# A two-layer graph attention kernel: the last head's aggregation in seven products, and layer 2's logits and softmax in another order

## The chip, the cores and the metric

The kernel runs on one core of a Trainium2 chip. The metric is the device time in microseconds. The engines that matter are TensorE (PE, matrix products; PEld is its weight load), VectorE (DVE), ScalarE (ACT), GpSimd (POOL, used here to issue accumulating DMAs) and SyncE (SP, which issues the plain DMAs). Each engine works through its own list of instructions in order.

## The reference

Everything is fp32. There are 512 nodes with 768 features, and 16,896 edges with self loops. `x` goes through two graph attention layers, and the result is the layer norm of `x` plus the second layer's output:

```python
def gat_layer(x, W, a_s, a_d, b, edge_index, concat):
    h = (x @ W).reshape(n, H, C)
    alpha_s = einsum('nhc,hc->nh', h, a_s)
    alpha_d = einsum('nhc,hc->nh', h, a_d)
    e = leaky_relu(alpha_s[src] + alpha_d[dst], 0.2)
    e = exp(e - segment_max(e, dst)[dst])
    alpha = e / (segment_sum(e, dst)[dst] + EPS)
    out = segment_sum(h[src] * alpha[:, :, None], dst)
    return out + b

h = elu(gat_layer(x, W1, ...))        # 8 heads of 768
out = gat_layer(h, W2, ...)           # 1 head of 768, from 8 x 768
x = layernorm(x + out)
```

The kernel turns the edge list into a 512 x 512 matrix of counts once, and then every attention is a dense softmax over 512 sources, with the counts folded in, followed by a dense product.

## The kernel before

**Stages.** A head of layer 1 has four: its projection (`x` times a 768 x 768 block of W1), its logits and softmax (which give `PT`, the transposed attention), its aggregation (the projected features times `PT`, then bias and ELU, which gives `gT`: 6 chunks of 128 features by 512 nodes), and its product with a 768 x 768 block of W2, which is added to `h2`, the features of layer 2. Heads overlap: while TensorE multiplies for one, VectorE and ScalarE do another's softmax. The loop over `h` ends with head 6, whose second product covers head 7's softmax. What stands behind the loop is head 7's aggregation and second product, then layer 2's logits, softmax, aggregation and layer norm, in one list.

**Products with fewer multiplications.** Most products are cut in two or three in each dimension and done in Strassen's manner, with sums of blocks ahead and sums of results behind. In halves there are seven products, P1 to P7, and four sums of blocks on each side. `mixed` does so for the aggregation of heads 0 to 6. It takes a pair of feature chunks (c and c+3) at a time: seven products of two matmuls of 128x128 by 128x256, in the order P1, P6, P7, P2, P5, P4, P3. P2 is added over P1's bank, P4 over P7's, P3 over P5's. ScalarE copies P1 into `u`; VectorE adds P6 to give the next `u`, P7 to give `w`, and makes both halves of `zr` and the last `u` from P5, P4 and P3. `elu` is three ScalarE instructions (Relu, Relu, Exp) and one on VectorE that writes `gT`. `left_sums` and `right_sums` make the sums for it. `second` does the last head's product with W2 in fourteen steps (seven products, two row tiles each), every step three matmuls of 384 columns, each with an emptying step: P1 goes to `u2` and P6 is added to it; P2, P7, P4, P5 and P3 go to `h2`; `fold` adds `u2` to the quarters of `h2` that want it.

**The last head** is aggregated plainly by `aggregate`: for each of six feature chunks, four matmuls of 128x128 by 128x512, and an ELU over all 512 nodes.

**Banks.** The pool `mm` has five banks of PSUM in rotation. A product that starts a bank waits until the engine that read the last one there is done.

**The order is written out by hand.** The program is scheduled manually: each engine runs its instructions in the order in which the Python issues them. In the loop, `plan` says what is issued behind the n-th of the fifteen products of `second_by_thirds` and ahead of its emptying: `score(t)` (lift: ScalarE spreads a tile's logits), `scored(t)` (`leak` and `rank` on VectorE, the exponential on ScalarE), `out_by_dma(t)` (scale, and a DMA transposition on SP's queue), `turn_in(t)` (ScalarE puts the transposed tile into `PT`). Tiles 2 and 3 of head 7 are transposed on TensorE by `turn`. Outputs in `by_dma` are emptied by ScalarE into a buffer of `pass_` or `absent` and added to `h2` by an accumulating DMA of POOL.

**Behind the loop, before.** `last_sum` (a POOL DMA) completes one weight sum of W2's last block. `right` gives two further sums, `t2` and `t4`, on VectorE. Eight logit rows of `h2` (`logits`, VectorE) lie between the aggregation's chunks. Layer 2's logits are linear in `h2`, so the last head's share comes from `V` times `gT` instead of from `h2`: `add_rows` multiplies two columns of weights by `gT`, in column tiles of TensorE 32 wide, up to four at a time, and adds `al2`, the logits of `h2` so far, in tile 2. `picks` spreads the resulting rows (`BC[H]`, `own`), and the softmax of layer 2 goes on beside the remaining ten products, one tile per two products. The last stage multiplies `PT` by `h2` for four node tiles, in two or three column pieces each, and VectorE adds the residual, takes the statistics and normalises.

Of the kernel before, what the change touches and what calls it, by code (L numbers as in the profile page):

```python
# [8 lines left out]
F32 = mybir.dt.float32  # L9
# [28 lines left out]
def gat_pass(  # L38
# [421 lines left out]
    def by_thirds(dest, A_, B_, order, fresh, by_dma=()):  # L460

        bank, begun, free = {}, set(), list(passed)

        def out(o):
            return dest[:, 2 * o[0]:2 * o[0] + 2, o[1] * TH:(o[1] + 1) * TH]

        def step(p):
            chain, o, sign = STEPS[p]
            copied = fresh and o not in begun
            begun.add(o)  # L470

            def multiply(between=None):
                first = chain not in bank
                if first:
                    bank[chain] = mm.tile([P, 512], F32, name="mm")
                for i in range(2):
                    for k in range(2):
                        if between and i == k == 1:
                            between()
                        nc.tensor.matmul(bank[chain][:, i * TH:(i + 1) * TH], A_[p][:, k, i * P:(i + 1) * P], B_[p][:, k, :],  # L480
                                         start=first and i == k == 0, stop=k == 1, skip_group_check=True)

            def empty():
                ps = bank[chain].rearrange("p (i n) -> p i n", i=2)
                if copied:
                    nc.scalar.activation(out(o), ps, AF.Copy, scale=sign)  # L486
                elif o in by_dma:
                    free.append(free.pop(0))
                    part = free[-1].rearrange("p (i n) -> p i n", i=2)
                    nc.scalar.activation(part, ps, AF.Copy, scale=sign)  # L490
                    nc.gpsimd.dma_start(out(o), part, accum_op=ALU.add)  # L491
                else:
                    nc.vector.tensor_tensor(out(o), out(o), ps, op=ALU.add if sign > 0 else ALU.subtract)  # L493
            return multiply, empty

        return [step(p) for p in order]
# [6 lines left out]

    def second_by_thirds(h, A_, B_):
        return by_thirds(h2, A_, B_, ("P13", "P2", "P8", "P4", "P12", "P9", "P6", "P0", "P1", "P14", "P10", "P5", "P11", "P7", "P3"),
                         False, ((1, 2), (0, 0), (0, 2)) if h + 2 < H else ((1, 2), (0, 0)))

    def second(A_, B_):

        bank = {}  # L510

        def pair(p, i, start, acc, new):
            def multiply(between=None):
                if start:
                    bank[i] = mm.tile([P, 512], F32, name="mm")
                product(bank[i], A_, B_, p, i, start, between)

            def empty():
                a, ps = acc(i), bank[i][:, :HALF]
                if new:  # L520
                    nc.vector.tensor_scalar(a, ps, 1.0, None, op0=ALU.mult)
                else:
                    nc.vector.tensor_tensor(a, a, ps, op=ALU.subtract if p == "P7" else ALU.add)
            return multiply, empty

        steps = [
            ("P1", True, lambda i: u2[:, i, :], True),
            ("P2", False, lambda i: h2[:, i, L], False),
            ("P6", True, lambda i: u2[:, i, :], False),
            ("P7", True, lambda i: h2[:, 2 + i, R], False),  # L530
            ("P4", False, lambda i: h2[:, 2 + i, L], False),
            ("P5", True, lambda i: h2[:, 2 + i, R], False),
            ("P3", False, lambda i: h2[:, i, R], False),
        ]
        return [pair(p, i, *rest) for p, *rest in steps for i in range(2)]
# [378 lines left out]
        nc.scalar.activation(neg, neg, AF.Exp, scale=-1.0)  # L914
        return lambda: nc.vector.scalar_tensor_tensor(gT[:, c, cols], neg, -1.0, pos, op0=ALU.add, op1=ALU.add)

    def aggregate(h, c):

        ps = mm.tile([P, 512], F32, name="mm")
        for s in range(NT):  # L920
            nc.tensor.matmul(ps[:, :N], HS[h][:, s, c * P:(c + 1) * P], PT[:, s, :],  # L921
                             start=(s == 0), stop=(s == NT - 1))
        return elu(h, c, ps[:, :N], slice(0, N), "r")

    near, far_ = slice(0, HN), slice(HN, N)

    def left_sums(h):
        hs = HS[h]  # L930
        a11, a12, a21, a22 = hs[:, :2, L], hs[:, 2:, L], hs[:, :2, R], hs[:, 2:, R]
        s1, s2, s4 = (gS.rearrange("p a k n -> p a (k n)")[:, j, :].rearrange("p (k n) -> p k n", k=2)
                      for j in range(3))
        tt = nc.vector.tensor_tensor
        return dict(P1=a11, P2=a12, P3=s4, P4=a22, P5=s1, P6=s2, P7=a21), [
            lambda: tt(s1, a21, a22, op=ALU.subtract),
            lambda: tt(s2, s1, a11, op=ALU.subtract),
            lambda: tt(a21, a11, a21, op=ALU.subtract),
            lambda: tt(s4, a12, s2, op=ALU.add),
        ]  # L940
# [12 lines left out]
    def mixed(h, A_, B_, fill, ends=()):  # L953
# [4 lines left out]
        def some(c, j):  # L958
            for f in fill[c][j]:
                f()  # L960

        for c in range(HK):
# [32 lines left out]
            for f in list(ends[1:]) * (c == HK - 1):  # L995
                f()
            tt(u, part("P3", over="P5"), u, op=ALU.subtract)
            some(c, 1)

            def others(c=c, u=u, zr=zr):  # L1000
# [116 lines left out]
    for h in range(H - 1):  # L1117
# [63 lines left out]
        else:  # L1181
# [27 lines left out]
            if last:  # L1209
                plan = {0: finish[:1], 1: finish[1:] + sum_up("P12") + at(score, 0), 2: sum_up("P9", "P7"), 3: sum_up("P1"),  # L1210
                        4: sum_up("P6") + at(scored, 0) + at(score, 1), 5: sum_up("P14"), 6: sum_up("P10") + at(scored, 1) + at(score, 2),
                        7: at(out_by_dma, 0) + sum_up("P5"), 8: sum_up("P11") + at(scored, 2) + at(score, 3), 9: at(out_by_dma, 1),
                        10: at(scored, 3), 11: at(scale, 2) + sum_up("P3"), 12: third_sum + at(scale, 3), 13: at(turn_in, 0) + at(turn_in, 1)}
            behind_it = {1: of_b("P7")}

            def also(n, *what):
# [55 lines left out]
        elif not last:  # L1272
            B_, sums = right(W1[h + 2], "w2")
            pairs = projection(h + 2, XA, B_)
            for n in range(14):
# [23 lines left out]
                if n == 13:  # L1299
                    late_["P10"]()  # L1300
                    behind = [late_["P8"]]
                    in_second, in_third = [late_["P13"], late_["P9"]], {2: late_["P12"], 7: late_["P5"]}
        else:
            last_sum()
            B2, sums2 = right(W2[H - 1], "w1")

# [3 lines left out]
    AL[H] = (al2[:, 0, :], al2[:, 1, :])  # L1312
    GA, gsums = left(gT, gS)
    nc.vector.tensor_tensor(V[:, :, 1], V[:, :, 1], V2, op=ALU.add)
    finish = []
    parts = [(h2[:, 2 + i, L], i, ALU.add) for i in range(2)] + [
        (h2[:, j + i, R], i, ALU.subtract) for j in (2, 0) for i in range(2)]

# [1 line left out]
        for part, i, op in parts:  # L1320
            nc.vector.tensor_tensor(part, part, u2[:, i, :], op=op)

    for c in range(DC):
        finish.append(aggregate(H - 1, c))
        if c:
            finish.pop(0)()
        if 0 < c < 5:
            logits(H, h2, c - 1)
        if c in (2, 4):
            sums2.pop(0)()  # L1330

    rows = tr.tile([P, 512], F32, name="tr")
    nc.vector.memset(rows, 0.0)

    def add_rows(lhsT, rhs, j, cols, start, stop):
        nc.tensor.matmul(rows[32 * j:32 * j + 2, cols], lhsT, rhs, start=start, stop=stop,
                         tile_position=(0, 32 * j), skip_group_check=True)

    every = slice(0, N)
    pairs = second(GA, B2)  # L1340
    pairs[0][0]()
    for c in range(4):
        add_rows(V[:, c, :], gT[:, c, :], c, every, True, c == 3)
    pairs[1][0]()
    pairs[0][1]()
    finish.pop(0)()
    for c in (4, 5):
        add_rows(V[:, c, :], gT[:, c, :], c - 4, every, False, True)
    for t in range(NT):
        add_rows(al2[:, :, t], ident, 2, slice(t * P, (t + 1) * P), False, t == NT - 1)  # L1350
    row2 = work.tile([P, N], F32, name="nr")
    nc.scalar.copy(row2, rows[:, :N])
    gsums[0]()
    gsums[1]()
    pairs[1][1]()
    pairs[2][0]()
    BC[H] = bc.tile([P, 512], F32, name="bc")
    nc.tensor.matmul(BC[H][:, :N], picks[:, 0:1].to_broadcast([P, P]), row2, start=True, stop=True)
    own = tr.tile([P, 512], F32, name="tr")
    for t in range(NT):  # L1360
        nc.tensor.matmul(own[:, t:t + 1], row2[:, t * P:(t + 1) * P], picks[:, 1:2], start=True, stop=True)
    gsums[2]()
    pairs[3][0]()
    gsums[3]()
    nc.vector.tensor_copy(own2, own[:, :NT])
    AL[H] = (None, own2)
    pairs[2][1]()
    pairs[3][1]()
    q, rden = [lift(H, 0)], []
    for n in range(2, 7):  # L1370
        (m0, e0), (m1, e1) = pairs[2 * n:2 * n + 2]
        m0()
        m1()
        if n < 6:
            leak(q[n - 2])
            rank(q[n - 2], n - 2)
        if n < 5:
            q.append(lift(H, n - 1))
        if n < 6:
            e0()  # L1380
        if n > 2:
            rden.append(weigh(q[n - 3], n - 3, scale=False))
            if n > 4:
                turn_in(n - 5)
            turn_out(q[n - 3], n - 3)
        if n == 6:
            fold(parts[2:4])
            e0()
        e1()
        if n == 2:  # L1390
            fold(parts[:2])
    fold(parts[4:])


# [71 lines left out]
```

## Time and profile before

| | |
|---|---|
| median of 3 runs | 634.85 us (634.31 to 635.33) |
| the profiled execution, its own time | 634.52 us |
| its span, first to last instruction | 632.7 us |
| TensorE busy | 621.1 us (98%) |
| VectorE busy | 520.1 us (82%) |
| ScalarE busy | 333.1 us (53%) |
| head 6's aggregation, seven products | 507.53 to 525.66 us |
| head 7's aggregation, plain | 552.97 to 573.84 us |
| its second product, with layer 2's softmax | 573.84 to 605.03 us |
| the last aggregation and layer norm | 605.03 to 632.7 us |
| granted TensorE clock, mean | 0.998 |

Times in the trace are microseconds from the start of the span. A row of the timeline has start, length, engine, line of the kernel, operation, output and inputs with their shapes, a count, and in brackets the engine's idle time before the row and what ended it. An fp32 matmul leaves two records, so 24 matmuls show as x48. Lengths of instructions in a queue overlap a little: the next one starts before the end of the last is recorded.

### The profile page before, as it was taken

The page shows a single profiled execution, that of the slowest core. Times are in us where ns is not written, and L with a number is a line of the kernel's source. Part 1 is how long each engine was busy: PE and PEld are TensorE (multiplying, and loading weights), DVE is VectorE, ACT ScalarE, POOL GpSimd, SP SyncE. Part 2 cuts the span into 40 slices and gives each one's busy share as a digit, 9 for nine tenths or more (in the row PEclk, how much of TensorE's full clock was granted, in tenths as well). Part 3 has the DMA queues.
Part 4 walks back from the last instruction along what each step waited for, and adds up shares of the span by engine and source line. Part 5 has one row for each costly group of instructions (what it writes and reads, how often), then busy time and mean ns, then how long its engine had stood idle before and what let it go on. Part 6 is the DMA issues. An engine that isn't in the chain of part 4 may idle for free.

```text
span 632.7 us, 8415 instructions
## 1 busy us (share of the span) xinstructions
PE 621.1 (98%) x2725; PEld 476.6 (75%) x2725; DVE 520.1 (82%) x1106; ACT 333.1 (53%) x585; POOL 148.6 (23%) x176
## 2 busy tenths in 40 slices
PE   8999999999999999999999999999999999999995
PEld 5555586556888888888888888888888888845553
DVE  8979989788898888968897878968896878756775
ACT  5874775640658246751658146751758056743440
POOL 1300011023342323323333432313342303110000
PEclk9999999999999999999999999999999999999999
DMA  8993397789999998999899998999899995270122
GB/s 307 327 235 91 73 256 254 174 240 264 235 209 155 317 256 184 188 275 222 225 225 201 295 249 199 172 286 239 209 219 217 284 283 86 51 179 1 33 59 79
DMA packets 108752, 127.36 MB, mean 201 GB/s; under 512 B 41574, under 2 KB 89886, under 8 KB 107934
## 3 DMA queue, kind: packets, MB, share of 16 engines
q1 hardware_dynamic: 74718, 90.17, 46.5%
q0 software_dynamic: 33552, 35.99, 37.2%
q10 hardware_dynamic: 432, 0.59, 0.3%
q8 instruction: 24, 0.39, 0.2%
q14 instruction: 26, 0.21, 0.1%
HBM read 98.66 MB, written 2.90 MB: 161 GB/s over the span
## 4 chain that ended last, share of the span: by engine, by line
PE 85%; DVE 7%; DMA 4%; ACT 2%; issue 1%; SPq 1%; DVEq 0%; POOLq 0%; ACTq 0%
PE mm L480 39%; PE mm L974 17%; PE mm L409 17%; PE mm L921 3%; PE mm L1412 3%; DMA w2r<-in_L_gnn_W_dram 3%; PE held L409 2%; PE tr L742 1%; DMA w2t<-in_L_gnn_a_dst_dram 1%; DVE h L493 1%; DVE q L640 1%; DVE q L645 1%; DVE hs L1073 1%; PE bc L276 1%; PE held L608 1%
## 5 line engine op out<-in xcount | busy, mean ns | idle before, releaser
L486 ACT ACTIVATE hs<-mm 128x512 f32<-128x512 f32 x30 | 17.9, 596 | 88.6 <-PE mm L480 70.5
L974 PE MATMUL mm<-PT,hs 128*128 128x256 f32 x252 | 61.3, 379 | 0.0
L493 DVE TENSOR_TENSOR hs<-hs,mm 128x512 f32<-128x512 f32 x45 | 30.8, 684 | 27.6 <-PE mm L480 27.6
L649 ACT ACTIVATE q<-q,nmax 128x512 f32<-128x512 f32 x32 | 23.1, 721 | 57.3 <-DVE nmax L645 57.3
L974 PEld LDWEIGHTS mm<-PT,hs 128*128 128x128 f32 x252 | 47.8, 190 | 7.2 <-ACT u L978 0.3
L491 POOL DMA_DIRECT2D h<-pass x23 | 27.7, 1313 | 94.7 <-ACT pass L490 85.8
L493 DVE TENSOR_TENSOR h<-h,mm 128x512 f32<-128x512 f32 x55 | 37.6, 684 | 9.6 <-PE mm L480 9.0
L974 PE MATMUL mm<-pS,gS 128*128 128x256 f32 x168 | 43.1, 379 | 0.0
L903 ACT COPY PT<-zr 128x1024 uint16<-128x1024 uint16 x34 | 39.1, 1155 | 2.4 <-DMA zr<-pS 1.8
L480 PE MATMUL mm<-w2r,gT 128*128 128x256 f32 x160 | 37.9, 385 | 0.0
L480 PE MATMUL mm<-w2r,xT 128*128 128x256 f32 x160 | 37.8, 379 | 0.0
L133 POOL DMA_DIRECT2D w1t<-in_L_gnn_W_dram x18 | 28.9, 1632 | 31.4 <-DMA w1t<-in_L_gnn_W_dram 29.6
L974 PEld LDWEIGHTS mm<-pS,gS 128*128 128x128 f32 x168 | 31.9, 190 | 4.3
L480 PE MATMUL mm<-w1t,hs 128*128 128x256 f32 x144 | 34.2, 380 | 0.5 <-DVE h L493 0.5
L480 PEld LDWEIGHTS mm<-w2r,gT 128*128 128x128 f32 x160 | 29.6, 190 | 6.6 <-DVE hs L493 3.0
L480 PE MATMUL mm<-w1r,hs 128*128 128x256 f32 x144 | 34.0, 379 | 0.0
L480 PE MATMUL mm<-w1r,gS 128*128 128x256 f32 x144 | 34.0, 379 | 0.0
L480 PEld LDWEIGHTS mm<-w2r,xT 128*128 128x128 f32 x160 | 30.4, 190 | 4.1
L978 ACT COPY u<-mm 128x256 f32<-128x256 f32 x21 | 7.8, 371 | 45.7 <-PE mm L974 45.7
L480 PEld LDWEIGHTS mm<-w1t,hs 128*128 128x128 f32 x144 | 27.2, 190 | 4.7 <-DVE h L493 0.9
L716 DVE TENSOR_SCALAR os<-nodes,idx 128x512 bf16<-128x512 f16 x104 | 29.0, 352 | 1.4 <-PE tr L742 1.4
L480 PEld LDWEIGHTS mm<-w1r,gS 128*128 128x128 f32 x144 | 27.3, 190 | 3.7
(282 smaller groups left out, 1544.8 us busy)
## 6 DMA issues: line engine op xcount, KB each, us to landing
w2r<-in_L_gnn_W_dram SPq DMA_DIRECT2D x48, 384.0 KB
w1r<-in_L_gnn_W_dram SPq DMA_DIRECT2D x43, 384.0 KB
gT<-xd SPq DMA_DIRECT2D x5, 1280.0 KB
w1t<-in_L_gnn_W_dram SPq DMA_DIRECT2D x24, 256.0 KB
h<-pass POOLq DMA_DIRECT2D x23, 256.0 KB, 4.7
w1t<-in_L_gnn_W_dram POOLq DMA_DIRECT2D x18, 256.0 KB, 6.1
w2t<-in_L_gnn_W_dram SPq DMA_DIRECT2D x15, 256.0 KB
w2t<-in_L_gnn_W_dram POOLq DMA_DIRECT2D x15, 256.0 KB, 8.9
```

What stands on the lines that cost most here:

```text
L133: nc.gpsimd.dma_start(o, i, accum_op=ALU.add)
L409: nc.tensor.matmul(ps[:, :HALF], A_[p][:, k, i * P:(i + 1) * P], B_[p][:, k, :], start=start and k == 0, stop=k == HK - 1, skip_group_chec ...
L480: nc.tensor.matmul(bank[chain][:, i * TH:(i + 1) * TH], A_[p][:, k, i * P:(i + 1) * P], B_[p][:, k, :], start=first and i == k == 0, stop= ...
L486: nc.scalar.activation(out(o), ps, AF.Copy, scale=sign)
L491: nc.gpsimd.dma_start(out(o), part, accum_op=ALU.add)
L493: nc.vector.tensor_tensor(out(o), out(o), ps, op=ALU.add if sign > 0 else ALU.subtract)
L649: nc.scalar.activation(q, q, AF.Exp, bias=nmax, scale=-1.0, accum_out=dens[t])
L716: nc.vector.tensor_scalar(o, nodes, idx[:, c:c + 1], None, op0=ALU.is_equal)
L903: nc.scalar.copy(PT.rearrange("p s n -> p (s n)").bitcast(U16).rearrange("p (s n h) -> p s n h", s=NT, h=2)[:, :, t * P:(t + 1) * P, :], p ...
L921: nc.tensor.matmul(ps[:, :N], HS[h][:, s, c * P:(c + 1) * P], PT[:, s, :], start=(s == 0), stop=(s == NT - 1))
L974: nc.tensor.matmul(bank[p][:, :HN], A_[p][:, k, c * P:(c + 1) * P], B_[p][:, k, :], start=over is None and k == 0, stop=k == 1, skip_group ...
L1412: nc.tensor.matmul(ps[:, :cols.stop - cols.start], PT[:, s, t * P:(t + 1) * P], h2[:, s, cols], start=(s == 2), stop=(s == 1))
```

## The change

The last head is aggregated by a new function, `last_mixed`, in seven products of halves for three pairs of chunks. It differs from `mixed` in the order. P1 of chunks 0 and 1 and P2 of chunks 0 and 1 come first, since they need no sums. Then P6, P7, P5, P4, P3 of chunk 0, the same five of chunk 1, and all seven of chunk 2 with P2 between P7 and P5. The four right sums and one left sum are issued on VectorE ahead of everything; the three other left sums are issued in the last steps of head 6's second product. One of them lies in `pass_`, and so head 6's output P7 no longer goes through `pass_` and a POOL DMA, but is added by VectorE.

The sums `t2` and `t4` of W2's last block are made by two loads on SP and two accumulating DMAs on POOL, as for the first heads (`sums_by_dma`). `second` empties P1 by a ScalarE copy instead of a VectorE one.

Layer 2's work is issued in another order. One logit row and then two are issued inside chunk 2 of the aggregation, the other five inside the second product. The six `gT` rows are issued together, in three column tiles, behind the third product; the `al2` rows behind the seventh product, alone; `picks` inside the eighth. The softmax starts behind the eighth product instead of the fourth.

```diff
-                elif o in by_dma:
+                elif p in by_dma:
...
-                         False, ((1, 2), (0, 0), (0, 2)) if h + 2 < H else ((1, 2), (0, 0)))
+                         False, ("P13", "P2", "P8", "P0", "P7", "P3") if h + 2 < H else ("P13", "P2", "P8", "P0"))
...
-                    nc.vector.tensor_scalar(a, ps, 1.0, None, op0=ALU.mult)
+                    nc.scalar.copy(a, ps)
...
-    def left_sums(h):
+    def left_sums(h, ends=None):
...
+        if ends is not None:
+            s2 = ends[:, :D].rearrange("p (k n) -> p k n", k=2)
...
+    def last_mixed(A_, B_, sums, fill):
+
+        h, tt = H - 1, nc.vector.tensor_tensor
+        banks, us, nears = {}, {}, {}
...
+        def begin(c):
+            us[c] = work.tile([P, HN], F32, name="u")
+            nc.scalar.copy(us[c], part(c, "P1"))
+
+        def near_half(c):
+            nears[c] = elu(h, c, part(c, "P2", "P1"), near, "l")
...
+        for f in sums:
+            f()
+        for c in range(2):
+            begin(c)
+        for c in range(2):
+            near_half(c)
+        behind = []
+        for c in range(HK):
+            if c == 2:
+                begin(c)
+            u, w, zr = us[c], work.tile([P, HN], F32, name="w"), work.tile([P, N], F32, name="zr", bufs=3)
+            if behind:
+                behind = behind[0]()
+            tt(u, u, part(c, "P6"), op=ALU.add)
+            if c == 0:
+                nears[0]()
+            tt(w, u, part(c, "P7"), op=ALU.add)
+            for f in behind[:1]:
+                f()
+            if c == 2:
+                near_half(c)
+            some(c, 0)
+            tt(zr[:, far_], part(c, "P5"), w, op=ALU.subtract)
+            for f in behind[1:]:
+                f()
+            tt(zr[:, near], u, part(c, "P4", "P7"), op=ALU.add)
+            if c:
+                nears[c]()
+            tt(u, part(c, "P3", "P5"), u, op=ALU.subtract)
+            some(c, 1)
...
-                        10: at(scored, 3), 11: at(scale, 2) + sum_up("P3"), 12: third_sum + at(scale, 3), 13: at(turn_in, 0) + at(turn_in, 1)}
+                        10: at(scored, 3), 11: at(scale, 2) + sum_up("P3"), 12: third_sum + at(turn_in, 0) + at(scale, 3), 13: at(turn_in, 1)}
+                AA, lsums = left_sums(H - 1, pass_.rearrange("p j n -> p (j n)"))
+                plan[13] += lsums[:2]
+                plan[14] = lsums[2:3]
...
+            B2, additions = sums_by_dma(W2[H - 1], w2[(H - 1) * D:, :], "w1")
+            additions[0]()
             last_sum()
-            B2, sums2 = right(W2[H - 1], "w1")
+            additions[1]()
...
-    for c in range(DC):
-        finish.append(aggregate(H - 1, c))
...
+    BB, rsums = right_sums()
+    finish = last_mixed(AA, BB, [*rsums, lsums[3]], {(1, 0): [lambda: nc.vector.memset(rows, 0.0)], (2, 0): second_[:1], (2, 1): first})
...
+    run(pairs[0][0], pairs[0][1], pairs[1][0], pairs[1][1], *finish, gsums[0], gsums[1], pairs[2][0], pairs[2][1])
+    for c in range(DC):
+        add_rows(V[:, c, :], gT[:, c, :], c % 3, every, c < 3, c > 2 and c % 3 != 2)
+    run(second_[1], pairs[3][0], gsums[2], pairs[3][1], *third_, pairs[4][0], *fourth, pairs[5][0], pairs[4][1], pairs[5][1], gsums[3],
+        pairs[6][0])
     for t in range(NT):
         add_rows(al2[:, :, t], ident, 2, slice(t * P, (t + 1) * P), False, t == NT - 1)
     row2 = work.tile([P, N], F32, name="nr")
     nc.scalar.copy(row2, rows[:, :N])
...
+    fold(parts[:2])
...
+    pairs[7][0](pick)
     nc.vector.tensor_copy(own2, own[:, :NT])
...
+    score(0)
+    run(pairs[6][1], pairs[7][1], pairs[8][0], pairs[9][0])
+    scored(0)
+    score(1)
+    pairs[8][1]()
+    weighed(0)
+    run(pairs[9][1], pairs[10][0], pairs[11][0])
+    scored(1)
+    score(2)
+    pairs[10][1]()
+    weighed(1)
+    scored(2)
+    score(3)
+    run(pairs[11][1], pairs[12][0], pairs[13][0])
+    turn_in(0)
+    weighed(2)
+    fold(parts[2:4])
+    scored(3)
+    pairs[12][1]()
+    turn_in(1)
+    weighed(3)
+    pairs[13][1]()
     fold(parts[4:])
```

In this list a step `pairs[n][0]` is a product, `pairs[n][1]` its emptying; `pairs[0]` and `[1]` are P1, `[2]` and `[3]` P2, then P6, P7, P4, P5, P3. `weighed(t)` takes the reciprocal of a tile's sum and sends the tile to its DMA transposition.

More of the change, by code (lines that the diff above doesn't have):

```diff
@@ L915, in elu @@
         return lambda: nc.vector.scalar_tensor_tensor(gT[:, c, cols], neg, -1.0, pos, op0=ALU.add, op1=ALU.add)
[L917 to L923, printed above, removed]
     near, far_ = slice(0, HN), slice(HN, N)
-    def left_sums(h):
+    def left_sums(h, ends=None):
         hs = HS[h]
@@ L997, in mixed, with others, part, some @@
             tt(u, part("P3", over="P5"), u, op=ALU.subtract)
+            some(c, 1)
+            def others(c=c, u=u, zr=zr):
+                return [elu(h, HK + c, zr, slice(0, N), "r", spare=zr), elu(h, c, u, far_, "l", spare=u)]
+            behind = [others]
+        return behind[0]()
+    def last_mixed(A_, B_, sums, fill):
+        h, tt = H - 1, nc.vector.tensor_tensor
+        banks, us, nears = {}, {}, {}
+        def part(c, p, over=None):
+            if over is None:
+                banks[c, p] = mm.tile([P, 512], F32, name="mm")
+            else:
+                banks[c, p] = banks[c, over]
+            for k in range(2):
+                nc.tensor.matmul(banks[c, p][:, :HN], A_[p][:, k, c * P:(c + 1) * P], B_[p][:, k, :],
+                                 start=over is None and k == 0, stop=k == 1, skip_group_check=True)
+            return banks[c, p][:, :HN]
+        def begin(c):
[3 more added lines that the diff above has]
+            nears[c] = elu(h, c, part(c, "P2", "P1"), near, "l")
+        def some(c, j):
+            for f in fill.get((c, j), ()):
+                f()
[23 more added lines that the diff above has]
+            for f in behind[1:]:
+                f()
+            tt(zr[:, near], u, part(c, "P4", "P7"), op=ALU.add)
+            if c:
+                nears[c]()
+            tt(u, part(c, "P3", "P5"), u, op=ALU.subtract)
             some(c, 1)
@@ L1314, in gat_pass @@
     nc.vector.tensor_tensor(V[:, :, 1], V[:, :, 1], V2, op=ALU.add)
-    finish = []
     parts = [(h2[:, 2 + i, L], i, ALU.add) for i in range(2)] + [
@@ L1321, in fold @@
             nc.vector.tensor_tensor(part, part, u2[:, i, :], op=op)
-    for c in range(DC):
-        finish.append(aggregate(H - 1, c))
[L1325 to L1330, printed above, removed]
     rows = tr.tile([P, 512], F32, name="tr")
-    nc.vector.memset(rows, 0.0)
     def add_rows(lhsT, rhs, j, cols, start, stop):
@@ L1337, in add_rows, with given, run @@
                          tile_position=(0, 32 * j), skip_group_check=True)
+    def given(t):
+        return [lambda al=al, a=a, sign=sign: nc.vector.scalar_tensor_tensor(
+            scr, h2[:, t, :], sign, a, op0=ALU.mult, op1=ALU.mult, accum_out=al[:, t:t + 1])
+            for al, a, sign in zip(AL[H], A[H], (1.0, -1.0))]
+    first, second_, third_, fourth = (given(t) for t in range(NT))
+    BB, rsums = right_sums()
+    finish = last_mixed(AA, BB, [*rsums, lsums[3]], {(1, 0): [lambda: nc.vector.memset(rows, 0.0)], (2, 0): second_[:1], (2, 1): first})
     every = slice(0, N)
     pairs = second(GA, B2)
[L1341 to L1348, printed above, removed]
+    def run(*fs):
+        for f in fs:
+            f()
+    run(pairs[0][0], pairs[0][1], pairs[1][0], pairs[1][1], *finish, gsums[0], gsums[1], pairs[2][0], pairs[2][1])
[3 more added lines that the diff above has]
+        pairs[6][0])
     for t in range(NT):
@@ L1352, in gat_pass, with pick, weighed @@
     nc.scalar.copy(row2, rows[:, :N])
[L1353 to L1358, printed above, removed]
-    own = tr.tile([P, 512], F32, name="tr")
[L1360 to L1364, printed above, removed]
+    fold(parts[:2])
+    own = tr.tile([P, 512], F32, name="tr")
+    def pick():
+        BC[H] = bc.tile([P, 512], F32, name="bc")
+        nc.tensor.matmul(BC[H][:, :N], picks[:, 0:1].to_broadcast([P, P]), row2, start=True, stop=True)
+        for t in range(NT):
+            nc.tensor.matmul(own[:, t:t + 1], row2[:, t * P:(t + 1) * P], picks[:, 1:2], start=True, stop=True)
+    pairs[7][0](pick)
     nc.vector.tensor_copy(own2, own[:, :NT])
     AL[H] = (None, own2)
[L1367 to L1391, printed above, removed]
+    q, rden = {}, {}
+    def weighed(t):
+        rden[t] = weigh(q[t], t, scale=False)
+        turn_out(q[t], t)
+    h = H - 1
+    score(0)
[20 more added lines that the diff above has]
+    pairs[13][1]()
     fold(parts[4:])
```

## The prediction

> **What bounds the kernel now.** I read the page first, then the chain of work that ended last, then the timeline around the last two heads.
>
> ```profile
> span 632.7 us, 8415 instructions
> ...
> PE 621.1 (98%) x2725; PEld 476.6 (75%) x2725; DVE 520.1 (82%) x1106; ACT 333.1 (53%) x585; POOL 148.6 (23%) x176
> ```
>
> TensorE is busy nearly all the time, so what counts is its work and the moments when it stands. The chain says where:
>
> ```profile
> 507.53 18.13 PE mm L974 x84
> ...
> 552.97 20.87 PE mm L921 x48
> 573.84 1.94 PE mm L409 x6
> 575.77 0.97 PE tr L1336 x8
> 576.75 2.13 PE mm L409 x6
> 578.88 0.98 PE tr L1336 x8
> 579.86 2.13 PE mm L409 x6
> 581.99 0.86 PE bc L1358 x2
> 582.85 0.79 PE tr L1361 x8
> 583.63 21.39 PE mm L409 x66
> 605.03 19.80 PE mm L1412 x64
> ```
>
> The columns are start, length, and what ran. One earlier head's aggregation, already in seven products (L974), is 18.13 us. The last head's, in plain form (L921), is 20.87. From 552.97 to 605.03, 52.06 us, the chain never leaves TensorE: aggregation, then fourteen products of layer 2 (L409, three matmuls each, 21.39/11 = 1.945 us where eleven follow each other), and the small matmuls of L1336, L1358 and L1361 between them. The last aggregation (L1412) follows at once. So in this stretch a microsecond off TensorE is a microsecond off the time, as long as VectorE and ScalarE, which empty its banks, keep up. These rows give their pace in head 6's aggregation:
>
> ```profile
> 510.82 1.03 PE L974 MATMUL mm<-pS,gS 128*128 128x256 f32 x4
> ...
> 511.69 1.03 PE L974 MATMUL mm<-pS,hs 128*128 128x256 f32 x4
> ...
> 511.89 0.42 DVE L990 TENSOR_TENSOR zr<-mm,w 128x256 f32<-128x256 f32 x1 [0.43 <-PE mm L974]
> ...
> 512.75 0.42 DVE L993 TENSOR_TENSOR zr<-u,mm 128x256 f32<-128x256 f32 x1 [0.44 <-PE mm L974]
> 513.09 0.42 DVE L915 SCALAR_TENSOR_TENSOR gT<-nl,zl 128x256 f32<-128x256 f32 x1
> ...
> 520.52 0.37 ACT L978 COPY u<-mm 128x256 f32<-128x256 f32 x1 [1.50 <-PE mm L974]
> 520.79 0.73 ACT L912 ACTIVATE nr<-zr,nb1T 128x512 f32<-128x512 f32 x1
> ...
> 522.82 0.69 DVE L915 SCALAR_TENSOR_TENSOR gT<-nr,zr 128x512 f32<-128x512 f32 x1 [0.15 <-ACT nr L914]
> ...
> 523.43 0.68 DVE L170 TENSOR_TENSOR w1r<-w1t,w1r 128x512 f32<-128x512 f32 x1
> ```
>
> Products follow each other at 0.87, or 18.13/21 = 0.863 us. VectorE reads a bank 0.20 after the next product's start (511.69 to 511.89), and its 256-wide rows follow each other 0.34 apart (512.75 to 513.09). A 512-wide row takes 0.61 until the next (522.82 to 523.43). ScalarE starts an ELU 0.27 after the copy `u`, and its result is taken 2.03 after that start (520.79 to 522.82).
>
> **The change part by part.**
>
> *Seven products instead of 24 wide matmuls.* 42 matmuls of 256 columns for 24 of 512: 18.13 for 20.87, so -2.74 us.
>
> *The start.* Three of the left sums move into head 6's last two products. One output of head 6 (P7) goes from ScalarE and a POOL DMA to VectorE, 0.6 us more there. `turn_in(0)` and `(1)` move up on ScalarE.
>
> ```profile
> 552.97 20.87 PE L921 MATMUL mm<-PT,hs 128*128 128x512 f32 x48 [0.28 <-ACT PT L888]
> ...
> 561.15 0.96 DVE L424 SCALAR_TENSOR_TENSOR scr<-h,w2t 128x768 bf16<-128x768 f32 x1 [1.93 <-DMA h<-pass]
> ...
> 562.15 0.96 DVE L424 SCALAR_TENSOR_TENSOR scr<-h,w2t 128x768 bf16<-128x768 f32 x1
> ...
> 573.02 0.69 DVE L915 SCALAR_TENSOR_TENSOR gT<-nr,zr 128x512 f32<-128x512 f32 x1
> ...
> 573.81 0.48 DVE L1333 MEMSET tr<- 128x512 f32 x1
> ```
>
> TensorE stood 0.28 us for a turned tile (first row; 0.4 counted from the last matmul's issue). P1 needs only tiles 0 and 1, so I take -0.4. The second P1 wants the bank that head 6's last product frees on VectorE, which I put at its due time: +0.05. The DMA that goes had a row of its own off the chain: nothing.
>
> *The sums beside the raw products.* P1 and P2 of chunks 0 and 1 cover 4 x 0.863 = 3.45 us, from about 552.55 to 556.0. VectorE has four 512-wide right sums (0.6 each) and one 768-wide left sum (0.87, an estimate: the 0.96 of such a row less the overlap of 0.08 that the shorter rows show), 3.3 us from 553.5 on. P6 at 556.0 needs the second (554.7), P7 at 556.9 the third, P4 at 558.6 the fourth (555.9), P3 at 559.5 the fifth (556.8). Nothing waits. Without the raw products ahead, up to 2 us would.
>
> *The joints in chunks 1 and 2.* P3 goes over P5's bank, so it waits until VectorE has read P5 into `zr`. In chunk 1, P7 ends at 562.0. VectorE then has `w` (562.25 to 562.6), gT of the chunk before (to 563.2), the memset of `rows` (0.48, with a lead of 0.19 after the ELU row in the rows above, to 563.8), and `zr` (to 564.25). P3 was due at 563.8: +0.5. In chunk 2, P1 ends at 566.0 and the copy `u` stands ahead of chunk 1's ELU on ScalarE, so that ELU runs 566.45 to 568.5. Then come gT (569.1), one logit (1.0, 561.15 to 562.15 in the rows), `zr` (570.5). P3 was due at 570.3: +0.25. Bounds: 0 if each VectorE row comes a third of a microsecond sooner, +1.5 for both together if the ELUs slip by their own 256-wide half. I take the walk, +0.75. The aggregation ends near 571.4.
>
> [...]
>
> *The copies of `u2`* go from VectorE (two of 0.56) to ScalarE, behind six ELU instructions of chunk 2: ready by 575.0, wanted at 575.3 by P2 over that bank. No cost, with 0.3 to spare; beyond it, one for one.
>
> *Two weight sums by DMA.* They take two 1.35 us rows off VectorE and put two loads on SP and two accumulations on POOL, one ahead of `last_sum` and one behind it; `last_sum` now waits behind the first one's load.
>
> ```profile
> w2r<-in_L_gnn_W_dram POOLq DMA_DIRECT2D x3, 576.0 KB, 13.6
> ...
> w1t<-w1t POOLq DMA_DIRECT2D x2, 576.0 KB, 9.2
> ```
>
> These are medians from issue to landing. A load from about 547, landing by 553 to 556, then 9.2, 13.6 and 9.2 one after the other even without overlap end near 588. The first is needed by P6 (581), the second by P7 (585, and it lands before 579), the third by P4 (592). The x rows behind the two loads on SP are wanted after 604. No cost; slack of 4 to 16 us.
>
> *The rows of logits.* Before, two batches (0.97, 0.98), the second holding four `al2` matmuls beside two wide ones. Now six wide ones in two rounds of three, about 1.83, and the four `al2` ones alone: 128 columns each, together as long as one 512 row, 0.86 (L1358), with a tenth for the change of tile. 2.8 for 1.95: +0.85. Bounds 0 (they overlap with neighbours after all) and +1.1.
>
> *Layer 2's logits and softmax.* The eight logit rows (1.0 each, five now inside the second product) and four gS sums fit: in 573.84 to 588, VectorE's list ends before 589. But the softmax starts four products later than before.
>
> ```profile
> 583.67 0.16 DVE L1365 COPY own<-tr 128x4 f32<-128x4 f32 x1 [2.46 <-PE tr L1361]
> 583.75 0.55 DVE L523 TENSOR_TENSOR h<-h,mm 128x384 f32<-128x384 f32 x1
> 583.87 0.69 ACT L636 ACTIVATE q<-bc,own 128x512 f32<-128x512 f32 x1 [3.34 <-DVE own L1365]
> ...
> 586.19 0.68 DVE L640 SCALAR_TENSOR_TENSOR q<-q 128x512 f32<-128x512 f32 x1
> ...
> 587.64 0.72 ACT L649 ACTIVATE q<-q,nmax 128x512 f32<-128x512 f32 x1 [3.08 <-DVE nmax L645]
> ...
> 588.36 0.67 ACT L636 ACTIVATE q<-bc,own 128x512 f32<-128x512 f32 x1
> ```
>
> Let X be the end of the `own` matmuls. Then `own2` is at X+0.2, the emptying `e6` X+0.3 to X+0.85, the first lift ends X+1.05. P4 goes over P7's bank and waits for `e6`, while TensorE has only the last third of the product that holds the picks (0.65): +0.25. From leak to exponential is 1.45 (586.19 to 587.64), from exponential to the next lift's end 1.39 (588.36 + 0.67 - 587.64). With `e7` first, leak 0 is at X+1.3, exponential 0 at X+2.75, leak 1 at X+5.45 (behind `e9`, whose product ends X+4.8), leak 2 at X+8.3, exponential 2 at X+9.75, lift 3 done X+11.15.
>
> ```profile
> 590.99 0.69 DVE L640 SCALAR_TENSOR_TENSOR q<-q 128x512 f32<-128x512 f32 x1
> ...
> 599.25 0.72 ACT L649 ACTIVATE q<-q,nmax 128x512 f32<-128x512 f32 x1 [1.55 <-DVE nmax L645]
> ...
> 599.97 1.14 ACT L903 COPY PT<-zr 128x1024 uint16<-128x1024 uint16 x1
> ...
> 610.23 0.62 DVE L1416 SCALAR_TENSOR_TENSOR hs<-mm,rden,hs 128x384 f32<-128x384 f32 x1 [0.51 <-PE mm L1412]
> ```
>
> `turn_in(0)` (1.14) then ends at X+12.3. TensorE reaches L1412 at X+0.65+0.25+6x1.945 = X+12.57. So the softmax stays just hidden, by 0.3, where it had several microseconds before. X itself: 571.4, three products (577.25), rows (579.2), 2.13 (the first product after rows, as 576.75 shows), three products (587.15), `al2` (588.1), two thirds of a product (589.6), 0.86 and 0.79: 591.25. L1412 starts at 603.8 instead of 605.03.
>
> *The tail.* Leak 3 comes at X+12, rank 3 ends X+13.4; two emptyings, the scalars and the last two folds end near X+16.2, `bias(0)` at X+17.1. TensorE's first bank is ready at X+15.35. So the first output row (L1416) is 1.75 us late.
>
> ```profile
> 624.85 0.48 DVE L1416 SCALAR_TENSOR_TENSOR hs<-mm,rden,hs 128x256 f32<-128x256 f32 x1 [0.49 <-PE mm L1412]
> ```
>
> VectorE idled 0.5 before the second piece of each of the four output tiles (first and last in the rows, 610.23 and 624.85), 2.0 in all, so the lag is made up just at the last one: no cost, with 0.2 to 0.3 to spare.
>
> *Sum.* -2.74 - 0.4 + 0.05 + 0.75 + 0.85 + 0.25 = -1.24 us. The profiled execution took 634.52, which gives 633.3; its median over the runs is 634.85, 0.33 higher, which gives 633.6. I take 633.5.
>
> **The rivals.**
>
> *The joints close.* VectorE runs a few tenths ahead and neither P3 nor P4 waits: -2.74 - 0.4 + 0.85 = -2.3, so 632.5. For it: in head 6 the same joints held with logits between them. Against: chunk 2's ELU now stands behind the copy of `u`.
>
> *The joints cost double* and both u2 and the softmax use up their 0.3: +0.75 more, 634.3, no change to be seen. For it: I count three places with 0.3 to spare.
>
> *The softmax becomes the bound* (slower). It has to fit four rounds between X and L1412, 12.5 us, where it had 21.4. In the rows of before, leak 0 to leak 1 took 4.8 us (586.19 to 590.99), and the fourth exponential came 11.6 after the first. I have 4.15 and about 10.7. Place: `fold` of the last weights behind the fourth rank, then the whole tail on VectorE, which has no idle time left to catch up. Its price is one for one beyond 0.3 us; it eats the gain at 1.5 and is slower by 0.2% from 2.8 late. If each of three rounds waits for one more product (1.945) than I have it, in part, 4 us late: 634.85 + 4 - 1.5 = 637.3; at 3 us late, 636.3. Against: the emptyings it queues behind come 1.945 apart and my walk has them.
>
> **How the numbers follow.** About 0.2% (1.27 us, below 633.58) is what a measurement of this kernel can tell from no change. The walk as it stands: 0.45, a little over half of it below that bound (0.25 faster, 0.20 the same). The joints close: 0.20, faster. The joints double: 0.13, 0.12 the same and 0.01 faster. The softmax: 0.22, slower. So 0.46 faster, 0.32 the same, 0.22 slower. The walk's own range is 632.9 to 634.1, its terms being good to 0.6. The whole range goes down to 632.3, which takes in the closed joints, and up to 636.2, which leaves out the later half of the last rival.
>
> **What would show it.** Right: 42 matmuls of 256 columns in about 19 us, with TensorE waits of 0.2 to 0.5 before P3 of chunks 1 and 2 released by VectorE's `zr`; four `al2` matmuls alone for 0.9 us; L1412 starting 1.2 earlier than 605.03; `own2` near 591; the end still a wait of VectorE for TensorE at the last cut tile. Wrong: a wait of L1412 for `PT`; VectorE without idle time between 604 and the end; a P6 or P4 product that waits for a DMA; P2 waiting for ScalarE's `u2`.

## The result, and the profile after

The changed kernel takes 633.37 us (median of 13 runs, 632.8 to 633.91) against 634.83 for the kernel before beside it: ratio 0.9978, 95% interval 0.9969 to 0.9986. Its profiled execution has a span of 631.6 us, 1.1 less than before, and took 633.37. The page:

```profile
span 631.6 us, 8545 instructions
...
PE 620.3 (98%) x2761; PEld 483.1 (76%) x2761; DVE 529.3 (84%) x1129; ACT 336.7 (53%) x598; POOL 149.2 (24%) x177
```

TensorE is busy 0.8 us less and as nearly always as before. The chain of the changed kernel answers to the one shown of before (start, length, what ran; `last_mixed` is L1008, the rows of logits L1384, the last aggregation L1472):

```profile
552.85 9.51 PE mm L1008 x44
...
562.39 0.42 DVE w L1039
562.81 0.61 DVE gT L915
...
563.52 0.48 DVE tr L1394
564.00 0.33 DVE zr L1045
...
564.37 7.42 PE mm L1008 x32
571.79 5.81 PE mm L409 x18
577.60 1.82 PE tr L1384 x12
...
587.36 0.96 PE tr L1384 x8
...
591.46 12.59 PE mm L409 x38
604.05 19.80 PE mm L1472 x64
```

The chain counts a piece of work from the end of the one before it. In it P1 starts at 552.85, right behind head 6's last matmuls, and the last aggregation at 604.05: 51.20 us. In the kernel before, head 6's last matmuls end at 550.80 + 1.89 = 552.69, and the aggregation starts at 552.97, behind its wait of 0.28:

```profile
550.80 1.89 PE L480 MATMUL mm<-w1r,hs 128*128 128x256 f32 x8
```

From 552.69 to the last aggregation at 605.03 it took 52.34 us. So the stretch is 1.14 us shorter. The two profiled executions differ by as much (634.52 and 633.37); the medians differ by 1.46, of which the interval allows 0.9 to 2.0. What the chain shows beside this is the one place where it leaves TensorE: from 562.39 to 564.33 it goes through `w`, gT, the memset and `zr` on VectorE.

The part ahead of head 7 differs from profile to profile by more than most of these terms. In the changed kernel's profile P1 starts at 552.85; in those of the experiments that leave the start alone, at 552.19 to 553.19. So below I compare stretches within one trace, and take the medians for the verdicts.

### The profile page after: what moved, and what is told of

The parts are those of the page before. It is cut to its first block, busy times and chain, and to the rows that moved or that the text cites. A ratio compares the mean times of both kernels' runs of the same rounds, so it can differ in the third digit from the quotient of the medians.

```text
span 631.6 us, 8545 instructions
## 1 busy us (share of the span) xinstructions
PE 620.3 (98%) x2761; PEld 483.1 (76%) x2761; DVE 529.3 (84%) x1129; ACT 336.7 (53%) x598; POOL 149.2 (24%) x177
## 4 chain that ended last, share of the span: by engine, by line
PE 88%; DVE 5%; DMA 4%; ACT 1%; issue 1%; SPq 1%; DVEq 0%; POOLq 0%; ACTq 0%
PE mm L480 42%; PE mm L966 17%; PE mm L409 17%; PE mm L1472 3%; DMA w2r<-in_L_gnn_W_dram 3%; PE mm L1008 3%; PE held L409 2%; PE tr L742 1%; DMA w2t<-in_L_gnn_a_dst_dram 1%; PE bc L276 1%; PE held L608 1%; PE bc L742 1%; DVE h L493 0%; PE tr L1384 0%; DVE q L645 0%
```

## The experiments

All times of the kernel before are those measured beside the experiment: 634.75 us for the first four, 634.40 for the next three, 634.44 for the last two.

**The last head aggregated plainly, all else changed.**

```diff
-    finish = last_mixed(AA, BB, [*rsums, lsums[3]], {...})
+    finish = []
+    for c in range(DC):
+        ps = mm.tile([P, 512], F32, name="mm")
+        for s in range(NT):
+            nc.tensor.matmul(ps[:, :N], HS[H - 1][:, s, c * P:(c + 1) * P], PT[:, s, :], start=s == 0, stop=s == NT - 1)
+        finish.append(elu(H - 1, c, ps[:, :N], slice(0, N), "r"))
+        if c:
+            finish.pop(0)()
+        for f in {2: [lambda: nc.vector.memset(rows, 0.0)], 3: second_[:1], 4: first}.get(c, ()):
+            f()
...
-                plan[13] += lsums[:2]
-                plan[14] = lsums[2:3]
```

> The changed kernel with the last head aggregated plainly again (24 matmuls of 512 columns, the three logit rows and the memset between its chunks); all the rest stays changed. If the seven products carry the gain: TensorE works 2.74 us longer and saves the two waits for zr (0.46 and 0.15 in the trace of the changed kernel), so the last aggregation starts about 2.1 us later than 604.05 and the time is about 635.5, slower than before. If the new order of layer 2 carries it: the time stays within 0.5 us of 633.4.

Measured: 634.81 us, ratio 1.0004 (0.9995 to 1.0013), the time of the kernel before. Its chain:

```profile
552.40 20.65 PE mm L1396 x48
...
605.30 19.80 PE mm L1479 x64
```

The aggregation is 20.65 us where the changed kernel has 18.94 (552.85 to 571.79). The whole stretch is 52.90 for 51.20. So the seven products are worth 1.7 us here and carry the gain; the other parts together bring nothing. That is less than the 2.1 expected: without the joints the products bring 20.65 - 18.13 = 2.52 and not 2.74, and the joints take 0.81 of it and not 0.61, as the next experiment shows.

**The joints.** The memset and the logit row leave the two joints.

```diff
-  {(1, 0): [lambda: nc.vector.memset(rows, 0.0)], (2, 0): second_[:1], (2, 1): first}
+  {(0, 1): [lambda: nc.vector.memset(rows, 0.0)], (2, 1): [second_[0], *first]}
```

> The changed kernel with the memset of rows moved from chunk 1 to the end of chunk 0, where VectorE stood 0.44 us, and the one logit row of chunk 2 moved behind its last product. If VectorE's queue is what holds P3 at the joints: TensorE's waits of 0.46 and 0.15 before P3 go, the last aggregation starts about 0.6 earlier (603.45) and the time is about 632.8. If the joints wait for ScalarE's ELU or for the banks instead: the waits stay, 633.4.

Measured: 632.45 us, ratio 0.9965 (0.9952 to 0.9977). Its chain:

```profile
552.59 18.13 PE mm L1008 x84
...
602.97 19.80 PE mm L1472 x64
```

The aggregation is now 18.13 us without a break, the length of the earlier heads'. So the joints cost 0.81, and VectorE's queue was their cause. The first is on the chain above. Both are in the timeline of the changed kernel (start, length, engine, line, operation):

```profile
563.05 1.03 PE L1008 MATMUL mm<-pS,hs 128*128 128x256 f32 x4
...
564.37 1.13 PE L1008 MATMUL mm<-PT,gS 128*128 128x256 f32 x4 [0.29 <-DVE zr L1045]
...
569.31 0.95 DVE L1388 SCALAR_TENSOR_TENSOR scr<-h,w2t 128x768 bf16<-128x768 f32 x1
...
569.65 1.03 PE L1008 MATMUL mm<-pS,hs 128*128 128x256 f32 x4
...
570.19 0.42 DVE L1045 TENSOR_TENSOR zr<-mm,w 128x256 f32<-128x256 f32 x1
...
570.66 1.13 PE L1008 MATMUL mm<-PT,gS 128*128 128x256 f32 x4
```

Without a wait a product starts 0.86 behind the start of the one before it; the rows overlap by the rest of their 1.03. In the first joint P4 starts at 563.05, so P3 was due at 563.91, and it starts at 564.37, behind `zr`. (The 0.29 in brackets is counted from the end of P4's row.) In the second P4 starts at 569.65, P3 was due at 570.51 and starts at 570.66, behind `zr`, which stands behind the logit row. The two delays are 0.46 and 0.15, 0.61 together. The other 0.2 lies in the products behind them: each row lasts 1.13 instead of 1.03.

**The rows of logits** in the batches of before.

```diff
-    for c in range(DC):
-        add_rows(V[:, c, :], gT[:, c, :], c % 3, every, c < 3, c > 2 and c % 3 != 2)
+    for c in range(4):
+        add_rows(V[:, c, :], gT[:, c, :], c, every, True, c == 3)
...
+    for c in (4, 5):
+        add_rows(V[:, c, :], gT[:, c, :], c - 4, every, False, True)
     for t in range(NT):
         add_rows(al2[:, :, t], ident, 2, slice(t * P, (t + 1) * P), False, t == NT - 1)
```

> The changed kernel with the rows of logits in the batches of before: four gT rows in four column tiles behind the third product, two gT rows together with the four al2 matmuls behind the seventh. If column tiles run beside each other and al2 alone costs its own length: L1384 takes about 1.95 us in all instead of 2.78, the last aggregation starts 0.8 earlier (603.2) and the time is about 632.6. If the al2 matmuls were hidden beside the full products: no change, 633.4.

Measured: 632.20 us, ratio 0.9963 (0.9949 to 0.9977). Its chain:

```profile
553.13 9.51 PE mm L1008 x44
...
577.87 0.97 PE tr L1384 x8
...
586.78 0.98 PE tr L1384 x8
...
603.48 19.80 PE mm L1474 x64
```

The batches take 0.97 and 0.98, where the changed kernel has 1.82 and 0.96. The second holds two wide rows and the four `al2` rows and is no longer than the `al2` rows alone. The stretch is 50.35, which is 0.85 less.

**All three**, with the emptying of P7's first bank ahead of `own2`.

```diff
     fold(parts[:2])
+    pairs[6][1]()
     own = tr.tile([P, 512], F32, name="tr")
...
-    run(pairs[6][1], pairs[7][1], pairs[8][0], pairs[9][0])
+    run(pairs[7][1], pairs[8][0], pairs[9][0])
```

> Both edits above together, and the emptying e6 issued on VectorE ahead of own2, so that P4's first product finds its bank free (it waited 0.25 us in the walk). If the three terms add up on TensorE: 0.6 + 0.8 + 0.25 = 1.65 us earlier, the last aggregation at 602.4, time about 631.7. If the softmax of layer 2 is the bound by then (turn_in(0) ended 0.28 us ahead of the last aggregation): part of it is lost, TensorE waits for PT, about 632.2 to 632.6.

Measured: 631.14 us, ratio 0.9948 (0.9934 to 0.9962): faster than both kernels. Its chain:

```profile
552.19 18.13 PE mm L1008 x84
...
589.15 12.36 PE mm L409 x38
601.51 19.80 PE mm L1475 x64
```

From P1 to the last aggregation it is 49.32 us, 1.88 less than in the changed kernel: 0.81 at the joints, 0.85 at the rows, and 0.23 in the last products (12.36 for 12.59). The terms add up, and the softmax does not become the bound. In the timeline `turn_in(0)` ends at 601.06 and TensorE uses it at 601.35, 0.29 later, as in the changed kernel (0.28, below). `own`, with which the softmax begins, moves with TensorE, and its second round starts behind an emptying that waits for a product:

```profile
593.81 0.55 DVE L523 TENSOR_TENSOR h<-h,mm 128x384 f32<-128x384 f32 x1 [0.75 <-PE mm L409]
594.28 0.69 DVE L640 SCALAR_TENSOR_TENSOR q<-q 128x512 f32<-128x512 f32 x1
```

**The softmax later.** Two idle ScalarE copies stand ahead of `turn_in(0)`.

```diff
+    for _ in range(2):
+        nc.scalar.activation(scr[:, :N], row2, AF.Copy)
     turn_in(0)
```

> The changed kernel with two more ScalarE copies of 128x512 (about 0.6 us each, their result unused) ahead of turn_in(0) of layer 2. If the softmax is hidden by only about 0.3 us: the last aggregation waits for PT and starts 0.8 to 1.0 us later (604.9 to 605.1), the time is about 634.3. If it has several microseconds to spare as before the change: no difference, 633.4.

Measured: 634.39 us, ratio 0.9998 (0.9989 to 1.0008). The wait of TensorE (total, times, longest), and its chain:

```profile
PE mm L1474 <- ACT PT L903: 0.8, 1, 0.8
```

```profile
602.80 0.53 ACT scr L1445
...
603.35 0.63 ACT scr L1445
603.98 1.06 ACT PT L903
...
605.09 20.07 PE mm L1474 x64
```

The two copies took 0.53 + 0.63 = 1.16 us, and TensorE waited 0.8 for the turned tile. So the softmax was hidden by about 0.4 us, counted from the end of TensorE's row before. In the changed kernel itself:

```profile
602.44 1.16 ACT L903 COPY PT<-zr 128x1024 uint16<-128x1024 uint16 x1
...
603.88 6.29 PE L1472 MATMUL mm<-h,PT 128*128 128x384 f32 x19
...
608.22 0.62 DVE L1476 SCALAR_TENSOR_TENSOR hs<-mm,rden,hs 128x384 f32<-128x384 f32 x1
```

`turn_in(0)` ends at 603.60 and TensorE uses it at 603.88: 0.28 us, counted to the start of TensorE's row.

**The sums first.** The products in the other heads' order.

```diff
-        for c in range(2):
-            begin(c)
-        for c in range(2):
-            near_half(c)
...
-            if c == 2:
-                begin(c)
+            begin(c)
...
-            if c == 2:
-                near_half(c)
+            near_half(c)
```

> The changed kernel with the products of the last head in the order of the other heads (P1, P6, P7, P2, P5, P4, P3 for every chunk), so that only one raw product covers the sums. If the raw products ahead hide the sums: TensorE waits about 1.3 us before the first P6 (for the second right sum), and saves the 0.46 of chunk 1, since P2 then lies between P7 and P5; the time is about 634.2. If the sums are hidden anyway: 633.0.

Measured: 634.19 us, ratio 0.9996 (0.9987 to 1.0005). Its wait:

```profile
PE mm L1008 <- DVE pS L940: 1.4, 1, 1.4
```

TensorE waits 1.4 us for the second right sum (L940). So the raw products ahead are a condition of the gain: with one of them only, the time is that of before within the interval.

**The sums and copies back on VectorE.**

```diff
-            B2, additions = sums_by_dma(W2[H - 1], w2[(H - 1) * D:, :], "w1")
-            additions[0]()
             last_sum()
-            additions[1]()
+            B2, sums2 = right(W2[H - 1], "w1")
...
-    run(..., *finish, gsums[0], gsums[1], pairs[2][0], pairs[2][1])
+    run(..., *finish, gsums[0], gsums[1], sums2[0], pairs[2][0], pairs[2][1])
...
     fold(parts[:2])
+    sums2[1]()
...
-                    nc.scalar.copy(a, ps)
+                    nc.vector.tensor_scalar(a, ps, 1.0, None, op0=ALU.mult)
```

> The changed kernel with the two weight sums back on VectorE (behind gsums[1] and behind the first folds, where it stood 0.6 and 2.7 us) and the two u2 copies back on VectorE; the two loads and two accumulations by DMA go. If moving them off VectorE bought nothing here, as the walk has it: within 0.3 us of 633.4, and L1384 starts at most 0.5 later. If VectorE in the second product is the bound: its list grows by 3.7 us and the time by 1 to 3 us.

Measured: 635.67 us, ratio 1.0023 (1.0013 to 1.0034). By the two ratios this is 0.45% or 2.9 us over the changed kernel, and it was not expected. In the profiles the last aggregation starts 2.3 us later (606.35 for 604.05). But most of the loss lies ahead of the second product. POOL's timeline and the chain of this kernel:

```profile
544.15 1.77 POOL L118 DMA_DIRECT2D w2r<-in_L_gnn_W_dram  x1
```

```profile
546.16 7.27 DMA zr<-pS
...
554.66 9.78 PE mm L1008 x44
```

`last_sum` (L118) is issued at 544.15. The transposition of head 7's tile 1, which starts in the chain at 546.16, lands 7.27 us later, at 553.43, and `turn_in(1)` and P1 wait for it. In the changed kernel the same `turn_in(1)` starts at 550.70, on ScalarE:

```profile
550.70 1.17 ACT L903 COPY PT<-zr 128x1024 uint16<-128x1024 uint16 x1 [0.70 <-DMA zr<-pS]
```

There POOL issues `last_sum` at 553.39, since it stands behind the first accumulation, which waits for a load until 552.80:

```profile
552.80 0.88 POOL L259 DMA_DIRECT2D w1t<-w2t  x1 [8.29 <-DMA w1t<-in_L_gnn_W_dram]
553.39 1.60 POOL L118 DMA_DIRECT2D w2r<-in_L_gnn_W_dram  x1
```

In the kernel before it stood behind the POOL DMA of output P7, which waited for ScalarE's copy until 552.75, as POOL's timeline of that kernel has it:

```profile
552.75 1.19 POOL L491 DMA_DIRECT2D h<-pass  x1 [8.40 <-ACT pass L490]
```

So a new theory: what costs is `last_sum` under way beside the transposition, and not VectorE's list. Two kernels test it.

**`last_sum` ahead of the first accumulation**, nothing else.

```diff
             B2, additions = sums_by_dma(W2[H - 1], w2[(H - 1) * D:, :], "w1")
-            additions[0]()
             last_sum()
+            additions[0]()
             additions[1]()
```

> The changed kernel with one swap on POOL's queue: last_sum is issued ahead of the first accumulation t2 += t1 instead of behind it, so it no longer waits for t2's load. If the loss of the kernel with the sums back on VectorE came from last_sum moving data while head 7's transposed tile is under way: last_sum is issued near 544 instead of 553, turn_in(1) waits for its transposition (553.4 there, 550.7 in the changed kernel), TensorE waits about 1.7 us before P1, and the time is about 635.2. If the loss came from VectorE's longer list: no difference, 633.4.

Measured: 635.78 us, ratio 1.0024 (1.0014 to 1.0034). POOL's timeline, the chain, and TensorE's wait:

```profile
544.08 1.77 POOL L118 DMA_DIRECT2D w2r<-in_L_gnn_W_dram  x1
```

```profile
546.09 7.24 DMA zr<-pS
...
554.56 9.78 PE mm L1008 x44
```

```profile
PE mm L1008 <- ACT PT L903: 1.7, 1, 1.7
```

The transposition takes 7.24 us, as with the sums on VectorE, and TensorE waits 1.7 for P1. One swap on a queue off the chain costs more than the whole change brings. The transposition took 7.27 and 7.24 us with `last_sum` under way, and 4.7 in the changed kernel (from 546.03, when ScalarE had filled its source, to 550.70). By what the one DMA holds up the other is not shown.

**`t4` and the copies on VectorE, `t2` still by DMA**, so that `last_sum` waits as in the changed kernel.

```diff
-            B2, additions = sums_by_dma(W2[H - 1], w2[(H - 1) * D:, :], "w1")
-            additions[0]()
+            t2 = w1_halves[2]
+            nc.sync.dma_start(t2, block(w2[(H - 1) * D:, :], 1, R))
+            nc.gpsimd.dma_start(t2, W2[H - 1][2], accum_op=ALU.add)
             last_sum()
-            additions[1]()
+            B2, sums2 = right(W2[H - 1], "w1")
```

(with `sums2[1]` and the `u2` copies on VectorE as above.)

> The changed kernel with t4 and the two u2 copies back on VectorE, but t2 still by a load and an accumulating DMA, so that last_sum still waits behind it on POOL. If only last_sum's early start cost time: within 0.3 us of 633.4, and no wait of TensorE before P1. If VectorE's 2.4 us more are what costs: 634.5 or more, with the loss behind 571.

Measured: 633.69 us, ratio 0.9987 (0.9978 to 0.9996). Its chain:

```profile
553.19 9.51 PE mm L1008 x44
...
572.13 6.03 PE mm L409 x18
...
604.61 19.80 PE mm L1474 x64
```

From P1 to the last aggregation it is 51.42, 0.22 more than in the changed kernel, and all of it in the first three products (6.03 for 5.81). It is not the copy itself that P2 waits for, but a row of gT behind it:

```profile
576.04 0.56 DVE L521 TENSOR_SCALAR pass<-mm 128x384 f32<-128x384 f32 x1 [1.10 <-PE mm L409]
576.51 0.68 DVE L915 SCALAR_TENSOR_TENSOR gT<-nr,zr 128x512 f32<-128x512 f32 x1
```

VectorE stands 1.10 us until it can copy the second bank of P1, and the gT row behind it, for which P2's third matmul has to wait, comes only then: the row ends at 577.19, and that matmul starts at 577.25. So the 2.4 us of VectorE work cost 0.2, and the rest of the loss above was the DMA.

## Why the prediction was right

633.5 us was predicted and 633.37 measured, and the sum of -1.24 us answers to -1.14 in the trace. Term by term:

- *Seven products, -2.74.* Right in mechanism; the size is 20.65 - 18.13 = 2.52 between two kernels without waits. The other 0.22 of the 20.87 belongs to the wait ahead of it: in the chain, a stretch that starts behind a wait is 0.27 longer than the same one without (9.78 for 9.51 where P1 waits for the transposition, 20.07 for 19.80 where the last aggregation waits for the softmax).
- *The start, -0.4.* Shown: in the changed kernel P1 follows head 6's last matmul without a wait. That takes away 0.28 of waiting and the 0.22 above, 0.50 in all. The two terms together were -3.14 and came to -3.02. The sum took the start from the issue of the last matmul and the aggregation from the chain, and so counted the overlap of two rows, 0.16, twice. The second P1 did not wait (predicted +0.05).
- *The DMA that goes.* "The DMA that goes had a row of its own off the chain: nothing" missed what stood behind it on POOL's queue. It had held `last_sum` back. The change put another wait there for a reason of its own, so that the result holds here is luck.
- *The sums beside the raw products.* No wait, and 1.4 us without the raw products.
- *The joints, +0.75.* 0.81 measured: 0.46 and 0.15 of delay where the walk had 0.5 and 0.25, and 0.2 in the longer rows behind, which the walk did not have. So the total is nearer than its parts. The 256-wide VectorE rows kept their 0.34 apart (570.19 to 570.53 is `zr` to gT), as in the rows of before.
- *The rows, +0.85.* 0.85 measured. (The walk to X gives the two rounds 1.95, from 577.25 to 579.2, where the term has 1.83; the trace has 1.82.)
- *P4's wait for `e6`, +0.25.* 0.23 measured.
- *The softmax hidden by 0.3.* About 0.4 by the added copies, 0.28 by the rows. The rival in which it becomes the bound did not come about: the rounds fitted as in the walk, and the combined kernel shows that they move with the products beside them.
- *The weight sums by DMA and the `u2` copies, no cost.* True in the changed kernel (P2 starts without a wait), and nearly as true of leaving them on VectorE, so they bring at most 0.2 themselves. What is worth about 2 us (the last aggregation starts at 606.02 for 604.05 with the swap; 0.46% by its ratio) is the first accumulation's place ahead of `last_sum`.
- *The tail.* The first output row starts at 608.22, about 1.6 behind TensorE, whose first bank is ready near 606.6 (an estimate: four matmuls of 0.645, from the 5.81 us of nine in the chain, starting at 603.88, and 0.2 until VectorE reads, as in head 6's rows), and the lag is made up. At the last tile VectorE waits for TensorE as before:

```profile
623.87 0.48 DVE L1476 SCALAR_TENSOR_TENSOR hs<-mm,rden,hs 128x256 f32<-128x256 f32 x1 [0.49 <-PE mm L1472]
```

Its idle time there is 0.49, as in the kernel before, where the walk left 0.2 to 0.3.

What stays open is from what time on `last_sum` no longer slows the transposition; only 544 and 553 were tried. It is also not shown what in `last_sum` does it, its bytes, its adding or its source.

## What to carry to other kernels

Where one engine bounds a stretch, walk the others' queues row by row to the places where it needs a bank back: the terms found so were good to about 0.2 us, and the three costs named could be taken away by edits (631.14 us with all three). A small independent row in another engine's queue held TensorE up here where it stood ahead of an emptying that frees a bank (0.46 of delay for the memset of 0.48, 0.15 for the logit row of 0.95); put it behind. Before removing a DMA or moving one on a queue, look at what it held back: the work behind it may start earlier and slow a transfer that someone is waiting for (7.24 us for 4.7 with the swap).

## What was not expected of the hardware

An accumulating DMA of 576 KB (`last_sum`) beside a DMA transposition stretched the latter from 4.7 us (546.03 to 550.70) to 7.3 and 7.2, in both kernels in which they met. A delay of TensorE of 0.15 us cost 0.25, and one of 0.46 cost 0.56: each first product behind it took 0.1 us more (1.13 for 1.03). Four 128-column matmuls in one column tile took as long alone (0.96) as with two 512-column ones in other tiles beside them (0.98).
